# Padding the rows of a routing table to a multiple of eight columns in a two-layer attention and mixture-of-experts kernel

## The chip, the cores and the metric

The kernel runs on one core of a Trainium2 chip. A core has five engines with a queue of instructions each: PE (TensorE, matrix products; its weight loads are listed apart as PEld), DVE (VectorE), ACT (ScalarE), POOL (GpSimd) and SP (SyncE), and 16 DMA engines that move data between HBM, the large memory, and SBUF, the core's own. The engines run side by side and wait for each other by semaphores. The metric is the device time of one execution in microseconds, as the median of several runs.

## The reference

Eight sequences of 512 tokens with 256 features go through two transformer blocks, all in float32:

```python
x = L0_attn_x                                   # (8, 512, 256)
x = x + _L0_attn_ref(_layernorm(x), Wq, Wk, Wv, Wo)        # causal, 16 heads of 16, 4 key heads, rotary
x = x + _L0_ffn_ref(_layernorm(x), router_w, w_gate, w_up, w_down)   # 32 experts of 96, the best 8
x = x + _L1_attn_ref(_layernorm(x), w_qkv, b_qkv, w_out, b_out)      # causal, 16 heads of 16
x = x + _L1_ffn_ref(_layernorm(x), gate_w, w1, w2, w3, sw1, sw2, sw3)  # 16 experts of 176, the best 2, and a shared one
```

An expert computes silu(t @ gate) * (t @ up) @ down on the tokens that chose it, times the token's weight for it. Which tokens choose which expert is known only while the kernel runs.

## The kernel before

**Stages.** The attention of layer 0 runs over the eight sequences; then the experts of layer 0, the attention of layer 1, and the experts of layer 1. A program part at the end recomputes everything in a general way if a check number is not zero; here it is only branched over.

**Routing.** After a sequence's attention, `route` picks the experts and POOL scatters each token's normed row, with its weights, into xg in HBM (L456): for every expert a slab. There are 4 x k scatters of 128 rows for a sequence, 32 in layer 0 and 8 in layer 1. They are put on a list, and `send(n, pace)` takes n of them from it: in `planned`, the loop of an attention, at every step of scores by SENT[layer] (L37); in the expert loop two at a step. In layer 1 these sends have no pace, that is, no further wait.

**Tables.** `tables` (L1065) cuts the slabs into tiles of 128 rows and makes, for every tile, its first row in xg and its expert. The first row goes to rowi, one row of numbers (L1077, L1149). From the expert's number come three offsets in offi, of three rows (L1078, L1154): j=0 where its gate and up weights start in SBUF, j=1 where its down weights start, j=2 the number itself. Both tiles lie on one partition, with four bytes a number. There are two parts. Part 0 holds the full tiles of the first sequences (4 in layer 0, 6 in layer 1), so that the experts can start early: 106 tiles in layer 0, 36 in layer 1. Part 1 holds the rest, 172 and 40 tiles. The tiles of SBUF are shared by both layers, so a row has 106 numbers in part 0 (the larger first count) and 288 in part 1.

**The expert loop.** `experts` takes two tiles at a step: `load` (SP brings their rows of xg into xg_m, L1244), four steps later `turn_x` (four transposes on PE, L1258, and a copy to SBUF on DVE, L1260), then `gate_up` (eight matmul rows of L1290, silu on ACT, the product on DVE, L1282), `turn_h` (L1309, L1310) and `down` (L1319, a copy on ACT, and the store of ys, L1327). In layer 1 DVE also makes to_m in `gate_up`, the numbers of the rows to which a result goes (L1270). Offsets come in registers: at every fourth step `load` first calls `registers`, which loads eight numbers of rowi on SP, eight each of the rows j=0 and j=1 of offi on PE, and eight of j=2 on DVE:

```python
RB = 8
...
    _, v = nc.values_load_multi_w_load_instructions(
        rowi[0:1, i:stop], engines=[ENG.SP], min_val=0, max_val=lay.end,
...
        nc.values_load_multi_w_load_instructions(
            offi[0:1, j, i:stop], engines=[eng], min_val=0, max_val=(lay.n_e - 1) * step,
...
        for j, (eng, step) in enumerate(((ENG.PE, lay.gu), (ENG.PE, w_dn), (ENG.DVE, 1)))
```

So PE's queue has, at every fourth step, two register loads in a row ahead of the transposes of that step. Other work is spread over the steps: in layer 0 the routing of the last sequence, the tables of part 1, the zero-fill behind the slabs' ends (32 transfers of SP, L1168), and late in the loop the first 64 gathers of results for layer 1 (POOL, L1399).

**The attention of layer 1** gathers its inputs: for a sequence POOL issues 32 indirect transfers that add the experts' results to the rows of x (L1399), 192 of them for the six sequences that the expert loop has not served.

**Order.** In both attentions and in the expert loop the order of PE's instructions is that in which the code records them (`manual_schedule`); that of the other engines comes from the framework's scheduler.

Of the kernel before, what the change touches and what calls it, by code (L numbers as in the profile page):

```python
# [10 lines left out]
I32 = mybir.dt.int32  # L11
# [22 lines left out]
PLAN1 = "cooggm oggm toggm coaggm aopggm taaoggm cppaoggm ppoggm taaopggm caopm aopam tapopm"  # L34
TAIL1 = "otaaoaaaoaoaoaa"
PB = (3, 2)
SENT = ((3, 3, 2), (2, 2, 2))  # L37
SPLIT = (4, 6)
AHEAD = 2
GU0, GU1 = ND * 2 * I0, ND * 2 * I1  # L40
# [58 lines left out]
def two_blocks_kernel(  # L99
# [116 lines left out]
    tpool = ctx.enter_context(tc.tile_pool(name="tiles", bufs=1, reuse_waits="tile"))  # L216
# [594 lines left out]
    def send(n, pace):  # L811
        for work, t, i in waiting[:n]:
            work(t, i, pace)
        del waiting[:n]

    def planned(att, before, after, plan, tail, ahead=None):
# [10 lines left out]
        for b in range(NB):  # L827
# [4 lines left out]
            for at, works in enumerate(plan.split()):  # L832
# [3 lines left out]
                att.scores(b, c, n, att.probs)  # L836
                send(SENT[att.n][n], None if att.n else att.newest)
                for work in works:
# [229 lines left out]
    def tables(lay, small, bank, part, beside=None, again=False):  # L1068

        n, n_e, name = lay.n, lay.n_e, f"{lay.n}{part}{'g' * again}"  # L1070
# [3 lines left out]
            start, stop = ((0, lay.n_first), (lay.n_first, lay.n_tiles))[part]  # L1074
        n_t, n_s = stop - start, n_e if again or part == 0 else 3 * n_e
        room = most if part else max(lay.n_first for lay in lays)
        rowi = tpool.tile([1, room], I32, tag=f"rowi{part}", name=f"rowi{name}")[:, :n_t]  # L1077
        offi = tpool.tile([1, 3, room], I32, tag=f"offi{part}", name=f"offi{name}")[:, :, :n_t]  # L1078
        lay.table[part] = rowi, offi
        count = small.tile([P, n_e], F32, tag="count", name=f"count_{name}", bufs=1)  # L1080
        nc.vector.tensor_tensor(count, lay.next, lay.slab, ALU.subtract)
# [465 lines left out]
    def all_experts(n, gw, gat, again=False, weights=()):  # L1547
# [6 lines left out]
        with ExitStack() as s:  # L1554
# [46 lines left out]
            if not again:  # L1601
                known = min(32 + begin, first - 4)
                beside.add(
                    begin, known, 6 + lay.n_e // 8, tables(lay, small, bank, 1, beside)
                )
# [24 lines left out]
    with ExitStack() as s2:  # L1630
        lasting.append(s2.enter_context(tc.tile_pool(name="xn_rows", bufs=2, reuse_waits="tile")))
        PARTS = 4
        with ExitStack() as s:
            awp, lnp, atp, late, ptp, smp, ps = pools(s, 0, False)
            bank = banks(ps, 3)
            att, before = fast0(awp, lnp, atp, late, ptp, ps, bank)
            route, _ = ffn_parts(smp, bank)
            gw0 = gpool.tile([P, E0 * GU0], F32, tag="gu", name="gw0")

            def after0(b):  # L1640
                if b == NB - 1:
                    return
                kept = keep_x(b, x_after[0])
                yield from routed0(b, lnp, bank, route)
                if b < PARTS:
                    with tc.issue_after(kept):
                        load_gate_up(gw0, f0, I0, N0, b, PARTS)
                if b == 1:
                    yield from biases1(smp, bank)
                if b == SPLIT[0] - 1:  # L1650
                    yield from tables(lays[0], smp, bank, 0)


            with tc.manual_schedule(engines={ENG.PE}):
                planned(att, before, after0, PLAN0, TAIL0)


        with ExitStack() as s1:
# [4 lines left out]
            with ExitStack() as s:  # L1663
# [15 lines left out]
                def after1(b):  # L1679
                    name = f"f1_{b}"  # L1680
                    xn = layernorm(xs[b], lnp, name, "xn_rows", 2, 2 * E1)
                    yield
                    xT = yield from turned(xn, lnp, bank, name)
                    yield from route(1, b, xn, xT, name, False)
                    yield from shared(w1["s"], xT, xs[b], name)
                    if b < SPLIT[1]:
                        keep_x(b, x_after[1])
                    if b == SPLIT[1] - 1:
                        yield from tables(lays[1], smp, bank, 0)
# [249 lines left out]
```

## Time and profile before

| | us |
|---|---|
| median of three runs | 1592.55 |
| the three runs | 1592.25, 1592.55, 1599.87 |
| the profiled execution | 1599.16 |
| its span, first to last instruction | 1597.4 |
| PE busy | 1429.2 (89%) |
| POOL busy | 805.5 (50%) |
| gathers of layer 1, L1399 | 256 of 1.576 us |
| gate and up products, L1290 | 1416 matmuls, 305.8 us |

The chain of waits, which is followed back from the last instruction, has PE for 49% of the span, POOL for 20% and 12% of "issue", time in which an engine waits for nothing that the profile shows. In the lists of waits a line names who waited, for whom, and then the total in microseconds, the number of times and the longest. In the timeline a line has start, duration, engine, source line, operation and tiles, the number of instructions merged, and in brackets the idle time before it with what ended it. Loads into registers are not counted as busy time of an engine; they are found by the tile that they read, on the sequencers (PEldq, DVEq, SPq), with shortest, median and longest duration in nanoseconds.

### The profile page before, as it was taken

The page shows a single profiled execution, that of the slowest core. Times are in us where ns is not written, and L with a number is a line of the kernel's source. Part 1 is how long each engine was busy: PE and PEld are TensorE (multiplying, and loading weights), DVE is VectorE, ACT ScalarE, POOL GpSimd, SP SyncE. Part 2 cuts the span into 40 slices and gives each one's busy share as a digit, 9 for nine tenths or more (in the row PEclk, how much of TensorE's full clock was granted, in tenths as well). Part 3 has the DMA queues.
Part 4 walks back from the last instruction along what each step waited for, and adds up shares of the span by engine and source line. Part 5 has one row for each costly group of instructions (what it writes and reads, how often), then busy time and mean ns, then how long its engine had stood idle before and what let it go on. Part 6 is the DMA issues. An engine that isn't in the chain of part 4 may idle for free.

```text
span 1597.4 us, 29845 instructions
## 1 busy us (share of the span) xinstructions
PE 1429.2 (89%) x9856; PEld 971.8 (61%) x9856; DVE 954.7 (60%) x3121; ACT 667.1 (42%) x885; POOL 805.5 (50%) x674
## 2 busy tenths in 40 slices
PE   5899999887888999999997899999798988999994
PEld 3455555545777889999863445545444454677773
DVE  5578888774555566555555657657465664544453
ACT  3566666562232223333324464664544642122221
POOL 0004777774545100365568888888888203233332
PEclk9899999998999999999998999999998988999996
DMA  2024554348778876899995556556454106353365
GB/s 78 14 67 133 170 167 165 120 140 233 254 230 258 264 231 201 216 253 243 256 234 83 70 71 122 112 86 135 80 87 102 45 15 186 102 170 114 113 211 188
DMA packets 230176, 240.36 MB, mean 150 GB/s; under 512 B 77916, under 2 KB 209377, under 8 KB 230018
## 3 DMA queue, kind: packets, MB, share of 16 engines
q1 hardware_dynamic: 173794, 148.87, 31.6%
q0 software_dynamic: 55872, 89.18, 24.6%
q8 instruction: 84, 1.38, 0.4%
q14 instruction: 74, 0.61, 0.1%
q10 hardware_dynamic: 352, 0.33, 0.1%
HBM read 127.36 MB, written 112.49 MB: 150 GB/s over the span
## 4 chain that ended last, share of the span: by engine, by line
PE 49%; POOL 20%; issue 12%; DVE 9%; ACT 5%; DMA 4%; SPq 1%; POOLq 0%; DVEq 0%; ACTq 0%
POOL x_a L1399 16%; PE gu_m L1290 15%; PE y_m L1319 10%; PE st_a L724 5%; PE xgT_m L1258 5%; PE o_a L747 4%; ACT p_a L729 4%; PE hT_m L1309 3%; POOL xg L456 2%; DMA xg<-xn_f,rows_f 2%; DVE p_a L735 2%; POOL yg L1332 1%; PE y_a L802 1%; PE sy_f L502 1%; DMA xg_m<-xg 1%
## 5 line engine op out<-in xcount | busy, mean ns | idle before, releaser
L1399 POOL DMA_INDIRECT x_a<-yg,yrows x256 | 403.5, 1576 | 255.8 <-DMA xg_m<-xg 125.5
L456 POOL DMA_INDIRECT xg<-xn_f,rows_f x320 | 322.4, 1007 | 374.3 <-ACT p_a L729 135.5
L729 ACT ACTIVATE p_a<-st_a 128x2048 f32<-128x2048 f32 (+1 forms) x192 | 306.1, 1594 | 260.2 <-PE st_a L724 151.0
L1290 PE MATMUL gu_m<-gw,xgTs_m 128*128 x1416 | 305.8, 360 | 0.0
L1290 PEld LDWEIGHTS gu_m<-gw,xgTs_m 128*128 128x128 f32 x1416 | 237.3, 194 | 24.7 <-DVE xgTs_m L1260 0.2
L724 PE MATMUL st_a<-qT_a,kT_a 32*128 32x512 f32 (+3 forms) x2048 | 202.6, 489 | 38.2 <-ACT p_a L729 31.1
L1319 PE MATMUL y_m<-dw,hTs_m 96*128 (+1 forms) x860 | 217.8, 383 | 2.3 <-issue 2.3
L735 DVE TENSOR_TENSOR p_a<-p_a,causal 128x512 f32<-128x512 f32 x256 | 170.4, 684 | 80.9 <-ACT p_a L729 80.7
L1260 DVE COPY xgTs_m<-xgT_m 128x512 f32<-128x512 f32 x177 | 121.8, 688 | 100.4 <-PE xgT_m L1258 100.2
L1324 ACT COPY ys_m<-y_m 128x512 f32<-128x512 f32 x177 | 103.6, 585 | 173.6 <-PE y_m L1319 158.4
L747 PE MATMUL o_a<-p_a,v 128*32 128x512 f32 (+3 forms) x2048 | 160.4, 452 | 10.8 <-DVE p_a L735 10.8
L724 PEld LDWEIGHTS st_a<-qT_a,kT_a 32*128 32x128 f32 x2048 | 89.1, 190 | 132.6 <-ACT p_a L729 58.4
L1319 PEld LDWEIGHTS y_m<-dw,hTs_m 96*128 96x128 f32 (+1 forms) x860 | 151.0, 192 | 16.7 <-issue 2.6
L1282 DVE SCALAR_TENSOR_TENSOR h_m<-h_m,xg_m,gu_m 128x96 f32<-128x96 f32 (+1 forms) x354 | 103.9, 325 | 82.0 <-ACT h_m L1295 38.5
L1332 POOL DMA_INDIRECT yg<-ys_m,to_m x76 | 76.4, 1006 | 140.4 <-ACT ys_m L1324 128.0
L747 PEld LDWEIGHTS o_a<-p_a,v 128*32 128x32 f32 x2048 | 57.9, 112 | 135.5 <-issue 98.7
L1258 PE MATMUL xgT_m<-ident,xg_m 128*128 128x128 f32 x708 | 110.5, 279 | 29.7 <-issue 16.7
L1310 DVE COPY hTs_m<-hT_m 96x256 f32<-96x256 f32 (+1 forms) x177 | 84.0, 475 | 81.4 <-PE hT_m L1309 81.4
L1298 ACT ACTIVATE h_m<-gu_m 128x192 f32<-128x192 f32 x139 | 45.9, 330 | 200.5 <-PE gu_m L1290 183.4
L1258 PEld LDWEIGHTS xgT_m<-ident,xg_m 128*128 128x128 f32 x708 | 87.4, 143 | 54.4 <-issue 31.9
L1309 PE MATMUL hT_m<-ident,h_m 128*96 128x128 f32 (+1 forms) x430 | 77.1, 275 | 0.1
L802 PE MATMUL y_a<-wo,oT_a 128*128 128x256 f32 x256 | 65.2, 401 | 11.0 <-DVE x_a L507 10.7
(242 smaller groups left out, 1635.7 us busy)
## 6 DMA issues: line engine op xcount, KB each, us to landing
xg_m<-xg SPq DMA_DIRECT2D x354, 144.0 KB
yg<-ys_m SPq DMA_DIRECT2D x139, 256.0 KB
g<-yg SPq DMA_DIRECT2D x16, 512.0 KB
xg<-zeros SPq DMA_DIRECT2D x50, 144.0 KB
xg<-xn_f,rows_f POOLq DMA_INDIRECT x320
x_after<-x_in SPq DMA_DIRECT2D x8, 512.0 KB
x_a<-x_after SPq DMA_DIRECT2D x8, 512.0 KB
x_a<-yg,yrows POOLq DMA_INDIRECT x256
```

Of the source, the lines that this page charges most:

```text
L456: inst = nc.gpsimd.indirect_dma_start(out=lay.xg, out_offset=bass.IndirectOffsetOnAxis(ap=rows[:, t, i : i + 1], axis=0), in_=xn[:, t, :], ...
L724: nc.tensor.matmul(st[:, g, at : at + T - j * P], kT[r, j * P : (j + 1) * P], qT[r, j * P :], start=True, stop=True,)
L729: self.newest = nc.scalar.activation(pt, st[:, :, :width], AF.Exp, scale=SCALE).ins
L735: self.masked = nc.vector.tensor_tensor(d, d, causal.unsqueeze(1).to_broadcast([P, NG, P]), ALU.mult).ins
L747: nc.tensor.matmul(o[32 * g : 32 * g + 32, j * P :], v1[:, j, v_at + g * (DH + 1) :][:, :32], probs[n][:, g, at : at + T - j * P], start=( ...
L1258: nc.tensor.transpose(tr[:, j, c, :], xg[:, j, c * P : (c + 1) * P], ident)
L1260: nc.vector.tensor_copy(xT, tr)
L1282: nc.vector.scalar_tensor_tensor(h[:, j, :], h[:, j, :], xg[:, j, D:][:, bass.ds(offs[part, i + j][2], 1)], gus[j][:, inner:], ALU.mult, A ...
L1290: nc.tensor.matmul(gus[j], xT[:, j, c, :], gu[:, bass.ds(at + c * 2 * inner, 2 * inner)], start=(c == 0), stop=(c == ND - 1),)
L1309: nc.tensor.transpose(hp[:n_in, q, j, :], h[:, j, lo : lo + n_in], ident)
L1319: nc.tensor.matmul(y[:, j, :], hT[:n_in, q, j, :], dn[:n_in, bass.ds(at + q * D, D)], start=(q == 0), stop=(q == n_ch - 1),)
L1399: inst = nc.gpsimd.indirect_dma_start(out=xs[b][:, t, :], out_offset=None, in_=lay.yg[: most_rows(b, again), :], in_offset=bass.IndirectOf ...
```

## The change

Two edits. The row length of rowi and offi is rounded up to a multiple of eight: 106 becomes 112 in part 0, 288 stays in part 1. The numbers used, their count and their instructions stay as they were; the rows j=1 and j=2 of offi start at another place in the tile, and the tiles that lie behind offi in SBUF move. And SENT of layer 1 goes from two scatters at a step to one.

```diff
-SENT = ((3, 3, 2), (2, 2, 2))
+SENT = ((3, 3, 2), (1, 1, 1))
```
```diff
         room = most if part else max(lay.n_first for lay in lays)
-        rowi = tpool.tile([1, room], I32, tag=f"rowi{part}", name=f"rowi{name}")[:, :n_t]
-        offi = tpool.tile([1, 3, room], I32, tag=f"offi{part}", name=f"offi{name}")[:, :, :n_t]
+        rowi = tpool.tile([1, -(-room // 8) * 8], I32, tag=f"rowi{part}", name=f"rowi{name}")[:, :n_t]
+        offi = tpool.tile([1, 3, -(-room // 8) * 8], I32, tag=f"offi{part}", name=f"offi{name}")[:, :, :n_t]
```

## The prediction

> **What bounds the kernel now.** I started from the table of windows, cut at the kernel's stages (columns: microseconds, then for each engine its busy time and instructions, granted TensorE clock, DMA share, GB/s).
>
> ```profile
> 394.00:408.24 14.24, 12.58 (x63) 11.18 (x64) 4.67 (x12) 3.04 (x7) 5.75 (x6) 0.76 0.69 226
> 408.24:546.55 138.31, 121.33 (x768) 109.10 (x767) 74.66 (x238) 40.70 (x87) 66.17 (x69) 0.98 0.78 250
> ...
> 566.00:660.00 94.00, 94.00 (x600) 87.59 (x599) 63.87 (x205) 30.32 (x67) 3.16 (x2) 1.00 0.75 213
> 660.00:815.00 155.00, 154.26 (x971) 141.28 (x970) 83.35 (x215) 49.32 (x108) 87.87 (x57) 1.00 1.02 250
> 815.00:1230.00 415.00, 369.23 (x2578) 195.91 (x2576) 251.75 (x785) 207.47 (x189) 343.96 (x228) 0.95 0.58 100
> ...
> 1366.00:1544.00 178.00, 175.22 (x854) 132.47 (x854) 86.22 (x235) 42.61 (x105) 64.15 (x66) 1.00 0.41 133
> ```
>
> The expert loop of layer 0 runs from 372 to 820. In its second part (566 to 815) PE is busy all the time: PE is the limit. In its first part (the full tiles, 408 to 546) the same loop leaves 17 us of PE idle. The attention of layer 1 (815 to 1230) is POOL's: 228 instructions in 415 us are one per 1.82 us, about a gather's 1.54 and the 0.30 between two. A delay before 815 moves that stage as a whole. So I asked the waits of 400 to 550 on PE who ends the 17 us (total, times, longest), and found one group:
>
> ```profile
> PE xgT_m L1258 <- issue: 16.7, 10, 4.0
> ```
>
> "Issue" means that PE waited for nothing that ends by a semaphore. Ten times in 138 us is once per four steps, the rhythm in which `load` calls `registers`. The view of the tile offi, asked about single loads and then by stage (count, shortest/median/longest in ns, first and last start):
>
> ```profile
> L1228 PEldq TENSOR_LOAD <-offi x1: 589/589/589, 435.6 to 435.6; - x1
> L1228 PEldq TENSOR_LOAD <-offi x1: 4891/4891/4891, 436.2 to 436.2; - x1
> ```
> ```profile
> L1228 PEldq TENSOR_LOAD <-offi x10: 334/802/2181, 1363.2 to 1418.6; - x10
> L1228 DVEq TENSOR_LOAD <-offi x4: 595/596/597, 1367.7 to 1397.3; - x4
> ```
> ```profile
> L1228 PEldq TENSOR_LOAD <-offi x10: 588/590/592, 1428.1 to 1508.4; - x10
> ```
> ```profile
> 436.63 0.60 PE L368 MATMUL xT_f<-ident,xn_f 128*128 128x128 f32 x4
> 441.20 1.09 PE L1258 MATMUL xgT_m<-ident,xg_m 128*128 128x128 f32 x4 [3.96 <-issue]
> 442.08 2.77 PE L1290 MATMUL gu_m<-gw,xgTs_m 128*128 x8
> ```
>
> PE loads two rows of offi, j=0 and then j=1, eight numbers each. In part 0 the first takes 0.59 us and the second 4.89; the matmuls queued ahead last until 437.24, and PE stands until the load ends at 441.14. In layer 1, whose transfers are fewer, it is the plain 590 against 1941 to 2181. In part 1 both rows take 590. What differs is where row j=1 starts: offi of part 0 has 106 columns, so it lies 424 bytes in, 8 past a multiple of 16 and of 32; part 1 has 288, so 1152 bytes, a multiple of 32. DVE reads row j=2, 848 bytes in, a multiple of 16 but not of 32, and is fast (596). So the slow case is a start off 16 bytes. The last four numbers of layer 1 fit: 334 ns from j=0, 1007 from j=1; the slow form grows by (1941 - 1007)/4 = 233 ns a number, as if read one by one.
>
> **The change part by part.**
>
> SENT. From (2, 2, 2) to (1, 1, 1) for layer 1. A sequence has 8 scatters, twelve steps of one still hold them, and they carry no pace. Built, both kernels have the same instructions in the same order on all five engines, with the same waits. Cost 0, nothing is moved, past no queue.
>
> rowi of part 0, 106 to 112 columns: its row starts at the tile's start either way, and SP's loads are fast (525 in quiet). 0.
>
> offi's copy (L1154) writes three rows of 106 instead of 318 in one run: once per layer, one partition, 0.3 us on DVE, well ahead of the first load. 0; without that cover at most 0.3 each.
>
> Row j=1 of offi: 424 becomes 448 bytes, j=2 becomes 896. The thirteen j=1 loads of eight in layer 0 sum to 36.3 us, their j=0 neighbours to 8.9, so 27.4 us of load time go there; in layer 1 four loads of 8.0 become 2.4. But it is PE's idle time that counts:
> - 408 to 524: eight stalls, of 1.76, 1.17, 3.96, 1.82, 1.07, 2.04, 1.18 and 1.34 = 14.3 us. They vanish wholly if both loads fit under what is queued: from the first load's start to PE's running dry it is 1.7 (435.56 to 437.24) to 2.5 us, two fast loads need 1.4 to 1.6, and part 1, with two fast loads every four steps, shows no such stall.
> - the clock: after the 3.96 us stall the granted clock is 0.5 from 439.1 to 445.9; eight gate-up matmuls take 2.56 us in the chain instead of 1.30. PE works 4.74 us of that, so 2.4 us come back.
> - 372 to 408: PE is idle 4.36, 2.33 and 1.61 us, but the first and last end with the landing of xg_m (the chain has that transfer until 381.76 and 397.05, within 0.2 us of the loads' ends), the middle one lies before the down weights, at a DMA share of 1.05 (370 to 394). I take 0; up to 6 if the loads alone held these.
> - 524 to 562: two stalls, 1.08 and 1.26. Here SP is the next to be late: from 524.7 it issues 32 zero-fill transfers (L1168, 0.55 us each with their registers, 18 us) among the loads of xg, it waits 1.4 us in all until 563, and PE waits for it at the end (waits of 524.5 to 563):
>
> ```profile
> PE xgT_m L1258 <- DMA xg_m<-xg: 3.7, 2, 2.9
> ```
>
>  SP can start no earlier by more than those 1.4 us, so of the two stalls' 2.3 between 0 and 1.4 is kept; I take 0.6, and the rest becomes a longer wait for xg_m at 551 and 558.
> - layer 1: in steady state the slow loads are hidden; from load to load four steps take 19.89 us with a slow one (1398.26 to 1418.15) and with fast ones (1428.10 to 1447.99). At the start four loads in a row stand before the first transpose, and PE idles 1.85 us. Its copy on DVE (L1260) stands behind to_m, done at 1368.80, and started at 1369.48: 0.7. I take 0.8.
>
> Sum: 14.3 + 2.4 + 0.6 + 0.8 = 18.1 us.
>
> **Rules weighed.** The Trainium skill, "Runtime: NRT & Kernel Launch", section Instruction fetch mechanics, prices a register load at about 200 ns per register even in bulk (there from HBM). By it eight numbers cost 1.6 us wherever a row starts, and a second load of 2.36 to 4.89 us shortens only to that: the eight stalls would give 12.0 us in place of 14.3, and the sum would be 15.8. The rows decide: 590 for eight is 74 ns each, 233 only in row j=1.
> A rule that speaks against the change: "DMA: Bandwidth & Descriptors", section How a descriptor splits into AXI transactions: reads begin at multiples of 256 bytes, and bytes in front are fetched unused. The longer offi moves nearly every later tile by 64 bytes. Where ys and xn_f lie, 32 past a 256 boundary becomes 96: a 1024-byte row goes from 33 to 35 beats of 32 bytes, an xn_f row of 1152 from 37 to 39, 5 to 6% more. No row of this trace shows this difference. Below, 0, because PE is busy 99.5% (154.26 of 155) at a share of 1.02, so no transfer ends PE's time there; above, 6% of these 155 us and of 24 at the start, 10.7 us, an estimate from that page. I take 0: the PE row is the nearer one.
>
> The profiled execution took 1599.16 us (span 1597.4), so it would become 1581.1. The median of the three runs, 1592.55, is 6.6 lower, and the other runs lie at 1592.25 and 1599.87; the saving is taken from the median: 1592.55 - 18.1 = 1574.5.
>
> **Rivals.**
> 1. Transfers take the place of the loads. 408 to 546 moves 138.3 us x 250 GB/s = 34.6 MB; the busiest long stage (370 to 394) did 268 GB/s, which needs 129 us. Saving 9.3 + 0.8: 1582.5. For: the stage must be squeezed to about 120 us. Against: its DMA share is 0.78, and PE is never seen waiting for xg_m in it.
> 2. The start of the row is not the cause (a second load right behind a first, or the hour of the transfers): nothing changes, 1592.5. Against: part 1 has the same pair at 590/590, and 1398.3 is slow in a quiet layer.
> 3. Slower: the 64 bytes make transfers dearer in both directions and DMA becomes the limit of the full-share stages (370 to 394, 660 to 815, 179 us). It decides from 18.1/179 = 10% longer packets; at 12% it costs 21.5: 1596. Against: PE's 99.5%, and the rule gives half of that, on one side.
>
> **How the numbers follow.** Forecast 83%, rival 1 10%, rival 2 4%, rival 3 3%. The forecast's own range is 1566 (6 from the start of layer 0, 2 more from the first transposes of layer 1 and run-to-run) to 1580. Reaching to rival 1, the range is 1565 to 1583. A change within 0.5% (8 us) can't be told from none here: faster is under 1584.6, which holds the forecast and most of rival 1 (0.92); same 0.05; slower 0.03.
>
> **What would show it.** Right: all PE loads of eight from offi at 0.59 to 0.9 us in part 0; the group "xgT_m <- issue" gone between 400 and 520; 408 to 546 shorter by 16 to 17 us; no half clock near 440; a longer wait for xg_m before part 1; POOL's stage of 415 us as long as before, only earlier. Wrong: the j=1 loads still near 1.9 us (rival 2), waits for xg_m in the middle of part 0 (rival 1), or PE idle in 660 to 815 (rival 3).

## The result and the profile after

| | before | after |
|---|---|---|
| median of six runs each, us | 1600.71 | 1578.68 |
| ratio, with its 95% interval | | 0.9869 [0.9826, 0.9912] |
| profiled execution, us | 1599.16 | 1575.68 |
| its span | 1597.4 | 1574.0 |
| PE busy | 1429.2 | 1423.1 |
| gate and up products, L1290 | 305.8 | 303.3 |
| POOL busy | 805.5 | 810.1 |

The change makes the kernel 1.3% faster; 23.5 us lie between the two profiled executions. One of the six runs after, 1847.67 us at a granted clock of 0.74, is in the median of 1578.68 but not in the ratio; the median of the other five is 1576.14. Two later comparisons, on two chips, gave 0.9845 [0.9807, 0.9883] and 0.9853 [0.9812, 0.9894].

First the table of windows of the changed kernel, cut at its own stages, with the columns of the table shown before (stretch, its length, busy time and instructions of PE, PEld, DVE, ACT and POOL, granted clock, DMA share, GB/s): part 0 of layer 0, the change of parts, part 1, the attention of layer 1, part 0 of layer 1.

```profile
407.76:526.48 118.72, 118.00 (x768) 107.53 (x767) 74.39 (x238) 40.79 (x87) 66.37 (x69) 1.00 0.88 287
526.48:560.50 34.02, 27.84 (x164) 24.65 (x163) 17.37 (x56) 8.22 (x19) 0.00 (x0) 0.95 0.79 246
560.50:777.40 216.90, 216.31 (x1370) 199.63 (x1369) 128.33 (x364) 69.68 (x153) 80.28 (x52) 1.00 0.91 235
794.00:1209.00 415.00, 372.43 (x2596) 199.40 (x2594) 249.85 (x785) 208.47 (x191) 343.50 (x227) 0.95 0.57 100
1341.70:1405.80 64.10, 62.60 (x308) 46.90 (x307) 31.98 (x103) 13.48 (x34) 17.77 (x18) 1.00 0.45 147
```

Part 0 has the same 768 matmuls as before in 118.72 us instead of 138.31, and PE is busy in 118.00 of them. PE's idle time fell from 17.0 us to 0.7, and the matmuls themselves take 3.3 us less, at a granted clock of 1.00 instead of 0.98. The transfers of the stage did not stretch it: the same data now moves at 287 GB/s instead of 250. Part 1 is as long as before, and POOL does the same 344 us of work in 415 us of attention, 21 us earlier.

These are all waits of PE from 400 to 526, the end of part 0 (who waited for whom, total, times, longest). The kernel before had ten waits of the group "issue" and 16.7 us there, from 400 to 550:

```profile
PE ro L1145 <- ACT ys_m L1324: 0.3, 1, 0.3
PE xgT_m L1258 <- issue: 0.2, 1, 0.2
PE gu_m L1290 <- DVE xgTs_m L1260: 0.2, 1, 0.2
```

And the loads of registers from the tile offi, in layer 0 from the first one to the end of part 0, then in layer 1 (count, shortest/median/longest ns, first and last start):

```profile
L1228 PEldq TENSOR_LOAD <-offi x28: 545/738/1416, 377.7 to 527.3; - x28
```
```profile
L1228 PEldq TENSOR_LOAD <-offi x18: 372/590/593, 1341.7 to 1466.1; - x18
L1228 DVEq TENSOR_LOAD <-offi x9: 344/597/599, 1346.1 to 1465.1; - x9
```

No load of PE is above 1.42 us in part 0 now, where row j=1 had reached 4.89. In layer 1, where fewer transfers run, none is above 0.593, where the loads of eight from row j=1 had taken 1.94 and more. The waits of PE from 524 to 562, the change of parts, show what PE waits for instead:

```profile
PE xgT_m L1258 <- DMA xg_m<-xg: 6.2, 5, 3.9
```

Before, the same line had 3.7 us in two waits. The stage is 2.3 us longer than before, against 19.6 won ahead of it.

### The profile page after: what moved, and what is told of

It is laid out like the page before. It is cut to its first block, busy times and chain, and to the rows that moved or that the text cites. A ratio compares the mean times of both kernels' runs of the same rounds, so it can differ in the third digit from the quotient of the medians.

```text
span 1574.0 us, 29845 instructions
## 1 busy us (share of the span) xinstructions
PE 1423.1 (90%) x9856; PEld 969.3 (62%) x9856; DVE 954.0 (61%) x3121; ACT 667.6 (42%) x885; POOL 810.1 (51%) x674
## 3 DMA queue, kind: packets, MB, share of 16 engines
q1 hardware_dynamic: 173794, 148.87, 31.8%
## 4 chain that ended last, share of the span: by engine, by line
PE 56%; DVE 12%; POOL 12%; issue 8%; ACT 6%; DMA 4%; SPq 1%; DVEq 0%; ACTq 0%; POOLq 0%
PE gu_m L1290 16%; PE y_m L1319 10%; POOL x_a L1399 9%; PE st_a L724 6%; PE o_a L747 5%; PE xgT_m L1258 4%; ACT p_a L729 4%; POOL xg L456 3%; PE hT_m L1309 3%; DVE p_a L735 2%; PE sg_f L489 2%; PE su_f L489 1%; PE sy_f L502 1%; PE y_a L802 1%; DMA xg<-xn_f,rows_f 1%
## 5 line engine op out<-in xcount | busy, mean ns | idle before, releaser
L456 POOL DMA_INDIRECT xg<-xn_f,rows_f x320 | 326.9, 1022 | 348.0 <-ACT p_a L729 134.5
L1290 PE MATMUL gu_m<-gw,xgTs_m 128*128 x1416 | 303.3, 358 | 1.1 <-DVE to_m L1270 0.9
L1290 PEld LDWEIGHTS gu_m<-gw,xgTs_m 128*128 128x128 f32 x1416 | 235.3, 192 | 26.1 <-DVE to_m L1270 1.2
L1319 PE MATMUL y_m<-dw,hTs_m 96*128 (+1 forms) x860 | 216.1, 381 | 3.0 <-issue 3.0
```

The costliest lines, as they stand in the source:

```text
L456: inst = nc.gpsimd.indirect_dma_start(out=lay.xg, out_offset=bass.IndirectOffsetOnAxis(ap=rows[:, t, i : i + 1], axis=0), in_=xn[:, t, :], ...
L1290: nc.tensor.matmul(gus[j], xT[:, j, c, :], gu[:, bass.ds(at + c * 2 * inner, 2 * inner)], start=(c == 0), stop=(c == ND - 1),)
L1319: nc.tensor.matmul(y[:, j, :], hT[:n_in, q, j, :], dn[:n_in, bass.ds(at + q * D, D)], start=(q == 0), stop=(q == n_ch - 1),)
```

## The experiments

All traces can be cut at the same places, the starts of PE's pairs of loads from offi, of which every kernel has 46. From one pair to the next is a group of four steps. In the table, "start" is the first three groups of layer 0; then come ten of part 0, three across the change of parts, nineteen of part 1, and the five of part 0 of layer 1 (us, one profiled execution each). The last column is the median of the timed runs and the ratio to before.

| kernel | start | part 0 | change of parts | part 1 | L1 part 0 | median, ratio [95%] |
|---|---|---|---|---|---|---|
| before | 32.5 | 138.3 | 31.8 | 217.4 | 64.9 | 1600.71 |
| after | 30.0 | 118.7 | 34.1 | 216.9 | 64.1 | 1578.68, 0.9869 [0.9826, 0.9912] |
| e8, the change | 30.1 | 118.4 | 33.7 | 217.0 | 64.1 | 1575.66, 0.9845 [0.9807, 0.9883] |
| e5, padding only | 31.0 | 118.1 | 35.9 | 216.3 | 64.1 | 1577.02, 0.985 [0.9808, 0.9893] |
| e6, rows of 107 | 32.0 | 158.7 | 30.3 | 216.5 | 67.1 | 1617.73, 1.0113 [1.0077, 1.015] |
| e7, POOL fills | 30.0 | 122.2 | 25.4 | 217.3 | 64.3 | 1572.1, 0.9835 [0.9797, 0.9872] |
| e12, the change | 28.2 | 120.1 | 33.2 | 216.6 | 64.1 | 1574.19, 0.9853 [0.9812, 0.9894] |
| e10, DVE slow | 31.2 | 130.2 | 31.7 | 216.7 | 68.2 | 1587.15, 0.993 [0.9914, 0.9947] |
| e11, POOL fills in layer 0 | 31.8 | 123.1 | 25.4 | 216.1 | 64.1 | 1567.34, 0.9802 [0.976, 0.9843] |
| e1, SENT only | 29.2 | 151.4 | 30.6 | 216.5 | 66.7 | 1706.75, 0.9991 [0.997, 1.0012] |
| e2, rows of 110 | 30.9 | 152.4 | 30.1 | 216.6 | 64.9 | 1707.61, 0.9999 [0.9976, 1.0022] |
| e3, rows of 108 | 28.6 | 133.5 | 32.9 | 215.7 | 64.1 | 1685.55, 0.9841 [0.978, 0.9902] |
| e4, part 1 slow | 27.9 | 131.8 | 35.4 | 254.0 | 64.1 | 1721.32, 1.0061 [1.0036, 1.0087] |

The last four (e1 to e4) ran together on a chip where the kernel before took 1708.48 us, 7% more than elsewhere, most of it gone already in the attention of layer 0, and part 0 was longer there too. They are compared only with each other and with that 1708.48. The others are compared with 1599.77 (e5 to e8) and 1598.99 (e10 to e12).

### Which of the two edits: e1 and e5

Each edit alone. e1:

```diff
-SENT = ((3, 3, 2), (2, 2, 2))
+SENT = ((3, 3, 2), (1, 1, 1))
```

> SENT of layer 1 at (1, 1, 1), rows of 106 as before. Theory (all of the gain comes from where row j=1 of offi starts, SENT moves nothing): the time of before within 0.3%, PE's loads of row j=1 in part 0 at 1.9 us and more, the group of PE waits xgT_m <- issue at 15 to 18 us between 400 and 550, the attention of layer 1 no shorter. Rival (SENT gives the part of the gain that lies in the attention of layer 1, where the changed kernel's trace is 3 us shorter): 3 us faster, with 540 instead of 543.5 us from the first transposes of layer 1's attention to its experts' first load.

Measured 0.9991 [0.997, 1.0012], with row j=1 still slow (36.1 us in all in layer 0's part 0). The interval alone would leave room for the rival's 3 us; but the traces of before and of e1 list the same instructions in the same order on every engine, so SENT has nothing to act by. e5 has the padding of the change and the old SENT:

```diff
 SENT = ((3, 3, 2), (2, 2, 2))
-        ... [1, room] ... [1, 3, room]
+        ... [1, -(-room // 8) * 8] ... [1, 3, -(-room // 8) * 8]
```

> The padding alone: rows of 112 columns, SENT of layer 1 back at (2, 2, 2). Theory (SENT does nothing): the changed kernel's time within 0.4%, ratio to before 0.984 to 0.989, and layer 1's attention as long as the changed kernel's on this chip within what it varies from run to run. Rival (SENT has a part of the gain): 0.2% or more slower than the changed kernel, all of it between the first transposes of layer 1's attention and its experts.

Measured 0.985 [0.9808, 0.9893], beside 0.9845 for the whole change in the same comparison. The padding makes the gain; SENT is worth nothing that shows.

### Start of a row, or the tiles moved behind it: e2 and e3

With rows of 110 every tile behind offi lies where the change puts it, but row j=1 starts 440 bytes in, 8 past a multiple of 16. With rows of 108 it starts at 432, a multiple of 16 and not of 32, and the tiles behind lie 32 bytes on instead of 64. Both have the new SENT.

```diff
-        offi = tpool.tile([1, 3, room], ...
+        offi = tpool.tile([1, 3, room if part else 110], ...     # e2; e3: 108
```

(and rowi in the same way.)

> The changed kernel with rows of 110 columns in part 0, which puts every other tile at the very address that it has in the changed kernel (64 bytes on), but starts row j=1 440 bytes in, 8 past a multiple of 16. Theory (the start of the row): the time of before, 1.2 to 1.4% above the changed kernel, loads of j=1 at 1.9 us in quiet. Rival (the moved tiles make it): the time of the changed kernel, loads of 0.6 us.

> Rows of 108 columns: row j=1 starts 432 bytes in, a multiple of 16 but not of 32; j=2 864 bytes in, a multiple of 32. Theory (16 bytes are enough, as row j=2 of before showed on DVE): loads of j=1 at 0.59 us in quiet and the changed kernel's time, ratio to before 0.986 to 0.989. Rival (it takes a multiple of eight columns, 32 bytes): loads of 1 us or more and part of the stalls, ratio 0.99 to 1.0.

The first five loads of PE in layer 1, from the view of the tile offi of e2, and the first six of e3; each list holds both rows, so that in e2 two of the five are of row j=1:

```profile
L1228 PEldq TENSOR_LOAD <-offi x5: 586/587/1943, 1465.4 to 1479.8; - x5
```
```profile
L1228 PEldq TENSOR_LOAD <-offi x6: 590/592/852, 1452.5 to 1466.8; - x6
```

Part 0 of e2 and of e3 in the table of windows, and then the largest waits of PE in it, one line of e2 and two of e3:

```profile
483.79:636.16 152.37, 126.83 (x760) 113.17 (x759) 74.15 (x238) 40.31 (x87) 66.61 (x69) 0.94 0.71 228
```
```profile
494.54:628.00 133.46, 122.10 (x760) 105.84 (x760) 72.92 (x238) 39.07 (x87) 66.81 (x69) 1.00 0.79 255
```
```profile
PE xgT_m L1258 <- issue: 23.8, 9, 3.8
```
```profile
PE hT_m L1309 <- DVE h_m L1282: 4.4, 7, 0.8
PE xgT_m L1258 <- issue: 2.7, 4, 1.0
```

In e2 the load of 1.94 us and the 23.8 us of "issue" are there as before, the clock is 0.94, and the time is that of before: moving the tiles does nothing, neither good nor harm. In e3 the group of "issue" has shrunk to 2.7 us, the clock is 1.00, and the ratio is the change's; part 0 is within 2 us of that of e4 on the same chip, where it has the change's 112 columns. So it is the start of the row that costs the time, and a multiple of 16 bytes is enough.

### The same slow loads where PE has no slack: e4

Rows of 290 in part 1 put its row j=1 off 16 bytes (1160, 8 past); part 0 is the change's.

```diff
+        ... [1, 3, 290 if part else 112]      # and rowi
```

> The changed kernel with rows of 290 columns in part 1, so that row j=1 starts 1160 bytes in, 8 past a multiple of 16: 22 loads of layer 0 and 5 of layer 1 become slow that were fast in both kernels. Theory (each slow load stands PE still by what it lasts beyond the queued matmuls, about 2.3 us from the start of the pair): loads of 1.9 to 3 us, a stall of about 1.2 us in each of 22 groups of part 1, 20 to 30 us more than the changed kernel, none of it in layer 1, where slow loads were hidden in steady state; ratio to before 1.000 to 1.007. Rival (PE's queue or another engine hides them in part 1): the changed kernel's time.

Part 1 of layer 0 in the windows, PE's waits in it, its loads there, and then those of part 1 in layer 1:

```profile
653.70:907.70 254.00, 226.63 (x1370) 206.02 (x1369) 129.79 (x364) 69.54 (x153) 80.24 (x52) 0.97 0.79 199
```
```profile
PE xgT_m L1258 <- issue: 21.1, 12, 2.7
PE xgT_m L1258 <- PE y_m L1319: 4.7, 6, 1.0
```
```profile
L1228 PEldq TENSOR_LOAD <-offi x37: 587/2258/3780, 654.5 to 895.6; - x37
```
```profile
L1228 PEldq TENSOR_LOAD <-offi x7: 589/2087/2108, 1573.0 to 1632.7; - x7
```

The stage grew from about 216 to 254 us, by 38 us, more than the 20 to 30 expected. PE's idle time is 27.4 us where e3 on the same chip has 0.5; that is 1.4 us for each of the 19 slow loads in this stretch, a little above the 1.2 expected. What the expectation left out is the clock: the same matmuls take 10 to 11 us more, at a granted clock of 0.97 instead of 1.00 (3% of 254 us would be 7.6). In layer 1 the same kind of load takes 2.1 us, and from the first to the last pair of loads part 1 lasts 79.58 us, within 0.01 of all other kernels: there it is hidden. The whole came out 0.6% slower, because part 0 keeps its gain.

### How far off, and which engine: e6 and e10

Rows of 107 put row j=1 12 bytes past a multiple of 16, and row j=2, which DVE reads, 8 past.

```diff
+        ... [1, 3, room if part else 107]     # and rowi
```

> Rows of 107 columns: j=1 starts 428 bytes in, 12 past a multiple of 16, and j=2, which DVE loads, 856 bytes in, 8 past one. Theory (what costs is PE's standing still; a start off 16 bytes is slow on any engine, number by number, whether it is off by 4, 8 or 12): PE's j=1 loads of eight at 1.94 us in quiet as with 106, DVE's j=2 loads at about 1.9 us instead of 0.6, and the time of before plus 0 to 0.4%, because DVE is busy for about half of part 0 and its stall of 1.4 us once in four steps is mostly idle time. Rival (DVE's loads are fast wherever they start): DVE 0.6 us. Rival (a start at a multiple of 4 but not of 8 bytes is slower still): PE above 2.5 us in quiet.

The loads of offi in layer 1's part 0 and its neighbourhood, then part 0 of layer 0 in the windows:

```profile
L1228 PEldq TENSOR_LOAD <-offi x14: 586/593/2181, 1380.6 to 1468.2; - x14
L1228 DVEq TENSOR_LOAD <-offi x7: 598/1847/2083, 1385.0 to 1467.1; - x7
```
```profile
411.54:570.28 158.74, 132.57 (x767) 116.84 (x766) 73.75 (x238) 40.73 (x87) 66.16 (x69) 0.92 0.69 222
```

Loads of row j=1 on PE take 1.94 us again in layer 1 (the 2.18 is the longest), so 12 bytes off is no dearer than 8. But DVE's, which took about 0.6 in layer 1 of every kernel so far, takes 1.85, and part 0 is 20 us longer than in the kernel before, where no difference above 0.4% was expected: that expectation was wrong. PE stands 26.2 us there (17.0 before), and at a clock of 0.92 its matmuls take 11.2 us more than before. Whether DVE's load does this alone was the question of e10: rows of 110, with the second and third row exchanged, so that PE's two rows start on 16 bytes and only DVE's does not.

```diff
-        for i, step in enumerate((lay.gu, dn, 1)):
+        for i, step in enumerate((lay.gu, 1, dn)):
...
-        for j, (eng, step) in enumerate(((ENG.PE, lay.gu), (ENG.PE, w_dn), (ENG.DVE, 1)))
+        for j, eng, step in ((0, ENG.PE, lay.gu), (2, ENG.PE, w_dn), (1, ENG.DVE, 1))
```

> Rows of 110 columns with the second and third row exchanged: PE's second load reads a row that starts 880 bytes in (a multiple of 16), DVE's load one that starts 440 bytes in (8 past one). So PE's loads are all fast and DVE's alone are slow, and every other tile is where the changed kernel has it. The 107-column kernel, where both were slow, took 1.1% more than before, 20 us more in part 0, which was not expected. Theory A (a slow load on DVE costs by itself: it comes behind a step's product and in front of the next one, PE's transposes of h wait for that, and PE's queue has less in it): part 0 of layer 0 at 130 to 138 us instead of 118.5, ratio to before 0.992 to 1.000. Theory B (DVE's stall costs only together with PE's, since PE then runs dry earlier in front of its own slow load): part 0 at most 122 us, the changed kernel's time within 0.3%, ratio 0.984 to 0.989.

The loads in part 0 and the change of parts, the largest wait of PE there, and one of these waits in the timeline:

```profile
L1228 PEldq TENSOR_LOAD <-offi x27: 544/622/1101, 407.5 to 569.3; - x27
L1228 DVEq TENSOR_LOAD <-offi x14: 765/2778/4109, 402.3 to 564.0; - x14
```
```profile
PE hT_m L1309 <- DVE h_m L1282: 6.8, 8, 1.3
```
```profile
430.61 0.31 DVE L1282 SCALAR_TENSOR_TENSOR h_m<-h_m,xg_m,gu_m 128x96 f32<-128x96 f32 x1 [2.72 <-ACT h_m L1298]
430.98 0.62 PE L1309 MATMUL hT_m<-ident,h_m 128*96 128x128 f32 x2 [1.28 <-DVE h_m L1282]
```

PE's loads are fast, DVE's take 2.8 us in the median, and PE now waits at `turn_h` for the product h_m of DVE. In the step shown, DVE's load ran from 427.54 to 430.36; ACT, to which the view puts DVE's 2.72 us, had been done at 430.11. All eight of PE's waits end 0.62 us behind such a load. Neither the kernel before nor the changed one had this wait at such a size (e3, on the slower chip, has 4.4 us of it with fast loads). Part 0 lasts 130.2 us, 10 to 12 more than the change: 7 to 8 us of that are idle time of PE, and the rest is longer matmuls at a clock of 1.00, for which no cause is shown. Part 0 of layer 1 grows by 4.1. With PE's row alone slow part 0 pays 20 us, with DVE's alone 10 to 12, with both 40. In these single profiles the two together cost more than their sum, and the granted clock is 0.92 with both, 0.98 with PE's alone and 1.00 with DVE's alone. By the medians it is 42 us against 24 and 13, which the intervals do not tell from a plain sum.

### What the change of parts gave back: e7, e11 and e12

In the changed kernel the waits for xg_m at the change of parts should go if SP did not have to issue the 32 zero-fill transfers. e7 gives them, with their registers, to POOL in both layers; e11 in layer 0 alone; e12 is the change again, for the comparison.

```diff
-            engines=[ENG.SP]
+            engines=[ENG.Pool]                  # e11: [ENG.SP if n else ENG.Pool], n the layer
...
-            nc.sync.dma_start(
+            nc.gpsimd.dma_start(                # e11: (nc.sync if n else nc.gpsimd)
```

> The changed kernel with the zero-fill behind the slabs' ends issued by POOL, whose queue is nearly empty then, instead of SP. Theory (SP's 32 zero-fills are why PE waits for xg_m at the change of parts, about 6 us in the changed kernel's trace and 3 us more than before): 3 to 7 us faster than the changed kernel, ratio to before 0.980 to 0.985, the waits of PE for xg_m at the change of parts gone or under 1.5 us. Rival (POOL's own scatters of the last sequence stand between the zero-fills and end later, and part 1 starts no earlier): the changed kernel's time or up to 0.5% more.

> As the kernel whose zero-fill is issued by POOL, but in layer 0 alone; in layer 1 SP issues it again, as in the changed kernel. The gain lies at layer 0's change of parts (25.4 instead of 34 us between the 13th and 16th group of loads), and the end of layer 1 took 3 us more there (91.8 instead of 88.5). Theory (that end was longer because POOL's zero-fills delay its scatters of results): 3 to 8 us faster than the changed kernel, ratio to before 0.979 to 0.983, the end at 88.5 to 90 us. Rival (the end varies by itself; or part 0 loses what the change of parts gains): within 3 us of the changed kernel.

> The changed kernel once more, for the comparison on the same chip. 0.983 to 0.988 of before.

Part 0 and the change of parts of e11 in the windows:

```profile
404.94:528.00 123.06, 118.98 (x768) 107.40 (x767) 74.12 (x238) 40.79 (x87) 84.54 (x102) 1.00 0.94 310
528.00:553.42 25.42, 25.42 (x164) 23.71 (x163) 17.19 (x56) 8.25 (x19) 0.00 (x0) 1.00 0.66 200
```

The change of parts is 25.42 us with PE busy in all of it, instead of 33 to 34 in e8 and e12: the waits for xg_m are gone, so SP's fill made them. Its issue has left this stage for part 0, and its transfers with it (the DMA share here is 0.66 instead of 0.79), so SP's queue and the transfers in the same stage are not told apart. POOL has 33 instructions more in part 0, which runs at a DMA share of 0.94 and is 3 to 4 us longer, so about 5 of the 8 us are left. In layer 1 the fill on POOL brings nothing that shows. From the last pair of loads to the end of the kernel it is 91.8 us in e7 and 87.8 in e11, as e11's theory has it, but also 91.4 in e12 and 88.5 in e8, where SP issues the fill of layer 1 as in e11: the end varies by itself. e11 has the lowest median, 1567.34 us against 1574.19 for the change and 1598.99 before. Its interval against before, [0.976, 0.9843], overlaps that of the change, [0.9812, 0.9894], so the 0.4% between these two is likely and not certain; e7 is 3.6 us below e8 in the same way.

## Why the prediction was right

The cause was the one named: row j=1 of offi starts off 16 bytes, its load of eight takes 1.94 us instead of 0.59 in layer 1 and up to 4.9 in layer 0, and PE stands behind it. Step by step:

- **The eight stalls of 408 to 524 (14.3) and the clock (2.4).** Right. With the two stalls of 524 to 546 that lie in this stage, part 0 became 19.6 us shorter, where 16 to 17 were forecast: the two stalls went there too, and what they gave was paid back only behind it. Of the 19.6 us, 16.3 are idle time and 3.3 shorter matmuls. The half clock explains 2.4 of these 3.3, and no half clock is left near 440; for the other 0.9 no cause is shown. The sign "all loads at 0.59 to 0.9 us" came nearly: 4 of the 26 loads of eight took 0.95 to 1.42 us, and PE stood behind none of them for more than 0.2.
- **The change of parts (0.6 of 2.3).** Right in kind: the longer wait for xg_m came, 6.2 us instead of 3.7, and the stage took back 2.3 us, all that the two stalls gave. From 408 to the end of the change of parts the net gain is 19.6 - 2.3 = 17.3, which is what 14.3 + 2.4 + 0.6 make. That it fits so well is luck: the idle time fell by 14.0 instead of 14.9, the matmuls by 3.3 instead of 2.4. e7 and e11 show that the zero-fill is the reason. (In the trace of before its first transfer leaves at 528.6; 524.7, which the prediction gives, is the start of SP's registers for the loads of xg ahead of it. No term of the sum rests on it.)
- **The start of layer 1 (0.8).** 64.86 became 64.09, and 64.1 to 64.3 in all later kernels whose rows in part 0 start on 16 bytes.
- **372 to 408 (0, up to 6).** The start became 2.5 us shorter. The seven other kernels with all rows on 16 bytes have 27.9 to 31.8, the five with a row off it 29.2 to 32.5, on two sorts of chip. The landing of xg_m still ends the longest wait (3.9 us). A part of the 2.5 may be the loads', but single profiles do not settle it.
- **SENT, the moved tiles, the copy of offi (0).** e1 shows the first and e2 the second. The bound of 10.7 us, the estimate from the Trainium skill, "DMA: Bandwidth & Descriptors", section How a descriptor splits into AXI transactions, was rightly not taken: at 0.9999 [0.9976, 1.0022] at most 4 us of it can hide in e2. Part 1, at a DMA share of 0.90 in both, lasts 216.5 us in e1 and 216.6 in e2, and its packets of 1024 bytes take 46 ns in the median and those of 1152 bytes 51, in both.
- **The price of a register.** By the Trainium skill, "Runtime: NRT & Kernel Launch", section Instruction fetch mechanics, about 200 ns each, the estimate would have been 15.8. The changed kernel shows 74 ns (590 for eight) on both rows. The page's figure, there for loads from HBM, is near the slow form only: 1941 for eight are 243 ns each, and 233 by the difference to a load of four, where the fast form has 64 by the same difference.
- **Rival 1** put the floor of part 0 at 129 us, from the 268 GB/s of the busiest long stage. Part 0 took 118.7 at 287 GB/s, and e11 went to 310: the rate of the busiest long stage of before was not a limit. **Rival 2** falls with e2 and e3, **rival 3** with e2.

The sum was too small. The profiled execution fell by 23.5 us, not 18.1. Besides the 17.3 and 0.8 there are 2.5 at the start, 0.5 in part 1, 3.2 in the attention of layer 1 and 1.2 in the tail, less 2.0 in the attention of layer 0. From the last loads of layer 0 to the first of layer 1, the attention of layer 1 takes 563.4 to 569.8 us in the kernels of the three comparisons off the slower chip: 567.5 before, 569.8 in e5, 563.7 to 564.8 in the three profiles of the whole change. The two longest are the two with the old SENT; but e5's median is not higher for it, on the slower chip four kernels with the new SENT spread over 575.9 to 582.6, and both values of SENT give the same instructions. So these last terms are counted as variation between executions and not as the change's, which is argued and not shown. Taken from medians, the saving is 22.0, 24.1 and 24.8 us. The interval of the first is 14 to 28 and holds 18.1; that of the second is 19 to 31 and does not, that of the third is 17 to 30. So the saving was likely a few us above the forecast, and where these arose is open. That 1574.5 and the measured 1578.68 lie only 4.2 apart is in part luck: the start, the median of three runs (1592.55), was 8.2 us too low against that of six (1600.71), and the larger saving made up for half of that.

## What to carry to other kernels

When an engine idles on "issue" at a fixed rhythm, look at the instructions that the busy time leaves out, register loads first, and compare the same instruction where it is fast with where it is slow: the address it reads was the only difference here. Pad the rows of a table from which registers are loaded so that every row starts on 16 bytes; here the moved tiles cost nothing that shows (e2). Every engine that reads such a row counts: DVE's row alone cost part 0 10 to 12 us, and 20 more where PE's was slow already. Slow loads that are hidden in one stage (79.58 us with or without them) cost 38 us in another, so they must be priced per stage by what is queued ahead of them.

## What the runs showed of the hardware

- In layer 1, a load of eight numbers from SBUF into registers takes 0.59 us on PE when its row starts at a multiple of 16 bytes (432, 448) and 1.94 us when it starts 8 or 12 bytes past one (424, 440, 428); on DVE it takes 0.60 against 1.85. Four numbers take 0.33 against 1.01 on PE. Starts 4 bytes past a multiple of 16 were not run. In the expert loop of layer 0, where the DMA share is 0.7 to 1.0, the slow form grew to 4.9 us (before), the fast one to 2.0 (e8, part 1).
- Slow loads cost the clock as well: in e4 the granted clock of part 1 fell from 1.00 to 0.97 with them; in e6, with both engines slow, that of part 0 was 0.92, and its 768 matmuls took 132.6 us instead of 118.0.
- DVE, busy 63% of part 0 in the changed kernel, still held PE up by its own loads alone (part 0 is 10 to 12 us longer in e10): the load that ended at 430.36 stood in its queue ahead of the product of 430.61, for which PE waited until 430.98.
